# A hybrid state-space and attention block: norms' Newton steps moved between engines, and one state's feed a step made by another engine

## The chip, the cores and the metric

The kernel runs on one core of a Trainium2 chip. A core has a matrix engine (PE, whose weight loads are listed as PEld), a vector engine (DVE), an activation engine (ACT), a general engine (POOL) and an engine that here only issues transfers (SP). Each works through its own instructions in the order in which the program lists them, and waits for others by semaphores. The metric is the device time of one execution in microseconds (us).

## What is computed

Eight pictures of 64 x 64 tokens with 96 channels go through two layers.

```python
# layer 0: group norm, then a four-direction state-space scan
xz = x @ in_proj_w.T ; xh, z = split(xz)
xc = silu(depthwise_conv3x3(xh) + conv_b)
xs = [diagonal, anti-diagonal, and both reversed]            # K=4 orders of the 4096 tokens
dts, Bs, Cs = split(xs @ x_proj_weight)
delta = softplus(dts @ dt_projs + bias)
def step(hst, inp):                                           # 192 channels, 16 states each
    u_t, d_t, B_t, C_t = inp
    hst = hst * exp(d_t[..., None] * A) + (d_t * u_t)[..., None] * B_t
    return hst, einsum(hst, C_t)
y = sum of the directions, in picture order, + Ds * xs
yn = layernorm(y) * ln_w + ln_b
x = x + yn * silu(z) @ out_proj_w.T
# layer 1: attention without a softmax, then a quantized feed-forward net
t = t + attention(layernorm(t))
t = t + ffn(layernorm(t))                                     # weights and inputs in 8-bit floats
```

## The kernel before

**Scan.** The 192 channels of two directions lie as three groups (g) of 128 partitions. A picture takes 16 steps: eight chunks of 512 tokens forward, then the same eight backward. A step runs over 16 states, so the main loop in `run` has 8 x 16 x 16 = 2048 turns, one state each. For a state n of a step m:

- `decay` (line 966): ACT makes exp(delta * A), three instructions, two turns ahead, into one of three buffers. A buffer is free again when DVE's scan three states before is done.
- the feed, delta * u * B, comes in one of three ways, by the letter in `FEED` for that state. For "A", ACT scales the transposed delta * u by B (line 988, eight instructions), and for "G" POOL does the same in three (line 979); both two turns ahead (`times_b`), into one of two buffers, and PE then transposes it with twelve matmuls into three PSUM banks (`turn`, line 996). For "D", PE spreads B's row over the partitions with one matmul (line 998), and DVE multiplies it by delta * u, three products (line 1013), just ahead of the scans.
- `recur` (line 1009): DVE scans the three groups. Between the second and the third scan it gives other work a place, `work.at("V")`.
- `keep` and `read` (lines 1025, 1030): one turn later POOL stores the carry and multiplies h by C.
- `reduce` (line 1044): four turns later PE adds it up over states and transposes it, in PSUM.

**Prologue of a step.** `prologue` makes delta, du (delta * u, line 928, POOL, one buffer) and its transpose duT for the step after next. du is made only when the step in hand has used the old one for the last time, which is told by `n == FEED.rindex("D")` in `recur`. The Softplus (line 921) needs another table in ACT, so two table loads go with it.

**Side work.** The stages before and after the scan of a picture run as jobs in the gaps of the main loop: `front` of picture b + 1 (norm, convolution, reordering) in the first half of picture b's steps, `measures` (group norm's statistics) of b + 2, and `tail` of b - 1 in the second half. A job is a generator; each `yield` names the engine of its next piece and a cost in us. `Work.at` lets a piece in when the engine's credit allows it; `LAGS` says how many turns must lie between pieces on different engines. After ACT, a POOL piece may go in the same turn ("AG": 0) and a DVE piece one turn later ("AV": 1); from POOL to PE, and from DVE to ACT, it is one turn, and from DVE to PE the last place of the same turn. In turn 7 of the next picture (`at == LAG + 3`) all that is left is issued at once.

**Tail.** For each of 8 chunks of 512 tokens, `join` adds the directions, takes a layer norm (n) that ACT applies, multiplies by the gate, projects, and takes a second layer norm (a), which POOL applies (lines 698 to 700), for attention's Gram matrix. When all are joined, `attention` makes one 96 x 96 matrix, and `layers` applies it, takes a third norm (f), which POOL applies (line 799), and runs the feed-forward net; its hidden values are cast to 8 bits by DVE (line 819). A chunk c is joined only when c - 2 is. The last picture's tail runs after the scans, all chunks side by side.

**Norm.** `rsqrt` (lines 395 to 412) gets mean and variance, takes variance to the power -1/2 by ACT's logarithm and exponential, and sharpens it by one Newton step on POOL (lines 405 to 411), which also gives -mean * r. Its tensors have 4 numbers a partition (one for each 128 tokens), or 1 for the group norm (line 466), whose results are copied to `at.norm`.

Of the kernel before, what the change touches and what calls it, by code (L numbers as in the profile page):

```python
# [13 lines left out]
ALU = mybir.AluOpType  # L14
# [6 lines left out]
DM = 96  # L21
# [23 lines left out]
DOUBLE = 2 * WW * DI  # L45
WIDE = 3 * WW * DI

FEED = "DADADAGADADAAAAA"


@with_exitstack
# [189 lines left out]
def dve(us, lag=None):  # L241
    return "V", us, lag, False


def gp(us, lag=None):
    return "G", us, lag, False
# [149 lines left out]
def rsqrt(nc, pool, k, mv, p, n, tag):  # L396

    r = pool.tile([p, n], F32, tag=tag + "r", name=tag + "r")
    s = pool.tile([p, n], F32, tag=tag + "s", name=tag + "s")
    m = pool.tile([p, n], F32, tag=tag + "m", name=tag + "m")  # L400
    yield act(0.4)
    nc.scalar.activation(r, mv[:, :, 1], AF.Ln, bias=k.eps[:p])
    nc.scalar.activation(r, r, AF.Exp, scale=-0.5)
    yield gp(1.0)
    nc.gpsimd.tensor_scalar(m, mv[:, :, 1], 1e-5, -0.5, ALU.add, ALU.mult)
    nc.gpsimd.tensor_tensor(s, r, r, ALU.mult)
    nc.gpsimd.tensor_tensor(s, s, m, ALU.mult)
    nc.gpsimd.tensor_scalar(s, s, 1.0, 1.5, ALU.mult, ALU.add)
    nc.gpsimd.tensor_tensor(r, r, s, ALU.mult)
    nc.gpsimd.tensor_tensor(m, mv[:, :, 0], r, ALU.mult)  # L410
    nc.gpsimd.tensor_scalar(m, m, -1.0, 0.0, ALU.mult, ALU.add)
    return r, m


# [13 lines left out]
def measures(tc, work, pool, x, k, at, b):  # L428

    nc = tc.nc  # L430
# [12 lines left out]
    def aggregate():  # L443
        mv = pool.tile([DM, 2], F32, tag="mv", name="mv")
        yield dve(0.4)
        nc.vector.bn_aggr(mv, stats.rearrange("p c s -> p (c s)"))

        ps = yield bank(0.1)
        v = view(ps, DM, 1)
        nc.tensor.matmul(v, k.group, mv[:, 0:1], start=True, stop=True)  # L450
        gmv = pool.tile([DM, 1, 2], F32, tag="gmv", name="gmv")
        yield act(0.2)
        nc.scalar.copy(gmv[:, :, 0], v)
        work.release(ps)
        dev = pool.tile([DM, 1], F32, tag="dev", name="dev")
        yield gp(0.6)
        nc.gpsimd.tensor_tensor(dev, mv[:, 0:1], gmv[:, :, 0], ALU.subtract)
        nc.gpsimd.tensor_tensor(dev, dev, dev, ALU.mult)
        nc.gpsimd.tensor_tensor(dev, dev, mv[:, 1:2], ALU.add)
        ps = yield bank(0.1)  # L460
        v = view(ps, DM, 1)
        nc.tensor.matmul(v, k.group, dev, start=True, stop=True)
        yield act(0.2)
        nc.scalar.copy(gmv[:, :, 1], v)
        work.release(ps)
        r, m = yield from rsqrt(nc, pool, k, gmv, DM, 1, "g")
        nc.gpsimd.tensor_copy(at.norm[:, 0:1], r)
        nc.gpsimd.tensor_copy(at.norm[:, 1:2], m)
        at.measured = True

    yield [aggregate()], 1
# [136 lines left out]
def tail(tc, work, x, out, k, at, b, last=False):  # L608


    nc = tc.nc
    area = dict(reuse_waits="tile")
    with tc.tile_pool(name=f"t1_{b}", bufs=1, **area) as p1:
# [5 lines left out]
        with tc.tile_pool(name=f"t2_{b}", bufs=8 if last else 2, **area) as p2:  # L619
# [3 lines left out]
            def join(c):  # L623
                s = slice(4 * c, 4 * c + 4)
# [69 lines left out]
                    nc.vector.bn_aggr(mv[:, i, :], st[:, i, :])  # L694
                r, m = yield from rsqrt(nc, p2, k, mv, P, 4, "a")
                xa = ys[0].rearrange("p a c -> p (a c)")[:, 0 : 4 * (DM + 1)].rearrange("p (a c) -> p a c", a=4)
                yield gp(1.6)
                nc.gpsimd.memset(xa[:, :, DM : DM + 1], 1.0)
                for i in range(4):
                    nc.gpsimd.tensor_scalar(xa[:, i, 0:DM], t[:, i, :], r[:, i : i + 1], m[:, i : i + 1], ALU.mult, ALU.add)  # L700


                ps = yield bank(0.65)
# [58 lines left out]
        with tc.tile_pool(name=f"t3_{b}", bufs=8 if last else 3, **area) as p2:  # L762

            def layers(c):
# [5 lines left out]
                if last:  # L770
                    t, xaT = kept[c]
# [22 lines left out]
                    nc.vector.bn_aggr(mv[:, i, :], st[:, i, :])  # L794
                r, m = yield from rsqrt(nc, p2, k, mv, P, 4, "f")
                xf = tile("xf", [P, 4, DM])
                yield gp(1.4)
                for i in range(4):
                    nc.gpsimd.tensor_scalar(xf[:, i, :], t[:, i, :], r[:, i : i + 1], m[:, i : i + 1], ALU.mult, ALU.add)

                ps = yield bank(0.45)
                v = view(ps, DM, CH)
# [477 lines left out]
```

## Time and profile before

| | us |
|---|---|
| median of 3 runs | 11244.71 (11232.78 to 11246.39) |
| profiled execution, span | 11243.9 |
| first scan of the loop | 244.2 |
| end of the last scan | 10996.3 |

Busy time over the whole span, of the lines that the change touches or stands next to:

```
L1009 DVE  scan h             6514.2 us in 5376, 879.5 us in 768
L966  ACT  decay              3975.0 us in 6144
L988  ACT  feedT              3673.7 us in 10240
L1044 PE   y                  3847.4 us in 24576
L928  POOL du                  448.4 us in 128
L1025 POOL carry               402.5 us in 2048
L799  POOL xf, scaling         107.0 us in 256
L700  POOL xa, scaling         106.1 us in 256
L405 to L411 POOL, norm f       96.9 us in 448
L405 to L411 POOL, norm a       89.3 us in 448
L405 to L411 POOL, norm n       89.1 us in 448
```

Busy time is the time in which at least one instruction of the group ran; where instructions overlap in the engine's pipeline, their mean duration times their number is more. A line such as "idle before, releaser" tells how long the engine stood still before these instructions and whose end let it go on.

### The profile page before, as it was taken

The page shows a single profiled execution, that of the slowest core. Times are in us where ns is not written, and L with a number is a line of the kernel's source. Part 1 is how long each engine was busy: PE and PEld are TensorE (multiplying, and loading weights), DVE is VectorE, ACT ScalarE, POOL GpSimd, SP SyncE. Part 2 cuts the span into 40 slices and gives each one's busy share as a digit, 9 for nine tenths or more (in the row PEclk, how much of TensorE's full clock was granted, in tenths as well). Part 3 has the DMA queues.
Part 4 walks back from the last instruction along what each step waited for, and adds up shares of the span by engine and source line. Part 5 has one row for each costly group of instructions (what it writes and reads, how often), then busy time and mean ns, then how long its engine had stood idle before and what let it go on. Part 6 is the DMA issues. An engine that isn't in the chain of part 4 may idle for free.

```text
span 11243.9 us, 182845 instructions
## 1 busy us (share of the span) xinstructions
PE 9140.0 (81%) x60885; PEld 7661.4 (68%) x60885; DVE 9396.9 (84%) x10582; ACT 9455.9 (84%) x19651; POOL 9365.4 (83%) x7047
## 2 busy tenths in 40 slices
PE   6888788878888788878888788887888878878884
PEld 5677677666676667766677666776667666666663
DVE  2988988888888888888888888888898888989993
ACT  3888888888888888888888888888898888888883
POOL 1877987899878998789987899779997799998994
PEclk8999999888998889988999898998999988889886
DMA  3335333543335443354334543345433543432332
GB/s 91 106 92 143 100 98 92 144 118 102 97 93 149 110 108 95 96 144 113 102 92 113 138 107 102 92 118 134 109 99 90 133 119 104 108 103 84 99 94 63
DMA packets 1122742, 1206.98 MB, mean 107 GB/s; under 512 B 452790, under 2 KB 730007, under 8 KB 1121799
## 3 DMA queue, kind: packets, MB, share of 16 engines
q1 hardware_dynamic: 1121798, 1195.28, 40.3%
q8 instruction: 485, 7.95, 0.3%
q14 instruction: 459, 3.75, 0.1%
HBM read 874.83 MB, written 319.98 MB: 106 GB/s over the span
## 4 chain that ended last, share of the span: by engine, by line
PE 24%; ACT 23%; DVE 17%; POOL 14%; issue 10%; DMA 7%; SPq 4%; DVEq 0%; POOLq 0%; ACTq 0%
DVE h L1009 11%; ACT feedT L988 9%; POOL h L1030 8%; ACT decay L966 7%; PE y L1044 7%; PE feed L996 7%; DMA cc<-crow 4%; DVE feed L1013 4%; PE bank L542 3%; SPq L587 2%; PE bank L894 2%; PE feed L998 1%; ACT L63 1%; POOL du L928 1%; DMA y<-wide 1%
## 5 line engine op out<-in xcount | busy, mean ns | idle before, releaser
L1030 POOL TENSOR_TENSOR h<-h,cc 128x1536 f32<-128x1536 f32 x2048 | 7079.9, 3457 | 458.3 <-DMA cc<-crow 228.9
L1009 DVE TENSOR_TENSOR_SCAN h<-decay,carry,feed 128x512 f32<-128x512 f32 x5376 | 6514.2, 1262 | 810.2 <-PE feed L996 704.8
L966 ACT ACTIVATE decay<-delta,a_neg 128x512 f32<-128x512 f32 x6144 | 3975.0, 714 | 1116.4 <-DVE h L1009 1114.4
L996 PE MATMUL feed<-ident,feedT 128*128 128x128 f32 x16896 | 3090.8, 303 | 1649.1 <-DVE h L1009 1084.6
L1044 PE MATMUL y<-ident,h 128*128 128x128 f32 x24576 | 3847.4, 290 | 130.7 <-POOL h L1030 47.4
L996 PEld LDWEIGHTS feed<-ident,feedT 128*128 128x128 f32 x16896 | 2209.1, 155 | 2246.9 <-ACT feedT L988 840.8
L988 ACT ACTIVATE feedT<-duT,rows 128x192 f32<-128x192 f32 x10240 | 3673.7, 445 | 17.6 <-PE feed L996 14.7
L1044 PEld LDWEIGHTS y<-ident,h 128*128 128x128 f32 x24576 | 3164.5, 152 | 525.2 <-issue 410.3
L1013 DVE TENSOR_TENSOR feed<-feed,du 128x512 f32<-128x512 f32 x1920 | 1200.4, 685 | 162.2 <-PE feed L998 146.5
L1025 POOL COPY carry<-h 128x3 f32<-128x3 f32 x2048 | 402.5, 197 | 877.0 <-DVE h L1009 803.2
L1009 DVE TENSOR_TENSOR_SCAN h<-decay,feed 128x512 f32<-128x512 f32 x768 | 879.5, 1201 | 118.9 <-PE feed L996 106.8
L542 PE MATMUL bank<-wf,xp 97*128 97x192 f32 x4266 | 851.9, 332 | 0.0
L998 PE MATMUL feed<-x,pick 77*128 77x512 f32 x1280 | 708.8, 636 | 3.9
L542 PEld LDWEIGHTS bank<-wf,xp 97*128 97x128 f32 x4266 | 692.8, 194 | 5.4 <-issue 4.6
L928 POOL TENSOR_TENSOR du<-delta,u 128x1536 f32<-128x1536 f32 x128 | 448.4, 3503 | 188.8 <-ACT delta L921 188.8
L916 PE MATMUL bank<-x,ws 13*128 13x512 f32 x764 | 435.5, 650 | 5.6 <-ACT x L907 5.6
L979 POOL TENSOR_TENSOR feedT<-duT,rows 128x512 f32<-128x512 f32 x384 | 396.2, 1060 | 4.7 <-PE feed L996 4.7
L894 PE MATMUL bank<-wx,u 128*128 128x77 f32 x3048 | 360.0, 275 | 0.0
L894 PEld LDWEIGHTS bank<-wx,u 128*128 128x128 f32 x3048 | 352.3, 193 | 1.9 <-ACT duT L936 0.2
L918 DVE COPY delta<-bank 128x512 f32<-128x512 f32 x382 | 256.7, 672 | 86.5 <-PE bank L916 86.1
L934 PE MATMUL bank<-ident,du 128*128 128x128 f32 x1532 | 251.8, 291 | 65.1 <-POOL du L928 61.8
L998 PEld LDWEIGHTS feed<-x,pick 77*128 77x128 f32 x1280 | 211.5, 200 | 97.6 <-DVE h L1009 44.8
(261 smaller groups left out, 6957.4 us busy)
## 6 DMA issues: line engine op xcount, KB each, us to landing
cc<-crow SPq DMA_DIRECT2D x4096, 128.0 KB
u<-seq SPq DMA_DIRECT2D x256, 384.0 KB
wide<-ys SPq DMA_DIRECT2D x512, 192.0 KB
ut<-image SPq DMA_DIRECT2D x768, 64.0 KB
seq<-us SPq DMA_DIRECT2D x128, 384.0 KB
part<-ys SPq DMA_DIRECT2D x64, 768.0 KB
y<-part SPq DMA_DIRECT2D x64, 768.0 KB
y<-wide SPq DMA_DIRECT2D x256, 192.0 KB
```

What stands on the lines that cost most here:

```text
L542: nc.tensor.matmul(v[:, j, :], flat[:, o : o + P], k.wf[:, i, :], start=(i == 0), stop=(i == 8), skip_group_check=True)
L894: nc.tensor.matmul(v[:, j, :], u[:, g, j * P : (j + 1) * P], w.wx[:, q, g, :], start=(g == 0), stop=(g == G - 1))
L916: nc.tensor.matmul(ps, w.ws[:, q, g, :], x[0 : 2 * NR + 1, :], start=True, stop=True)
L928: nc.gpsimd.tensor_tensor(du, delta, u, ALU.mult)
L966: nc.scalar.activation(decays[i][:, g, :], made[m].delta[:, g, :], AF.Exp, scale=w.a_neg[:, q, g, n : n + 1])
L988: nc.scalar.activation(f[part], o.duT[part], AF.Copy, scale=o.rows[:, j, XB + d * NS + n : XB + d * NS + n + 1])
L996: nc.tensor.transpose(feed[g][:, j * P : (j + 1) * P], feeds[i][:, j * G + g, :], w.ident)
L998: nc.tensor.matmul(feed[0], w.pick[:, FEED[:n].count("D"), :], made[m].x, start=True, stop=True)
L1009: nc.vector.tensor_tensor_scan(h[:, g, back], a[:, g, back], feed[g][:, back], init, ALU.mult, ALU.add)
L1013: nc.vector.tensor_tensor(feed[g], feed[0], made[m].du[:, g, :], ALU.mult)
L1030: nc.gpsimd.tensor_tensor(hs[i], hs[i], c.unsqueeze(1).to_broadcast([P, G, T]), ALU.mult)
L1044: nc.tensor.matmul(y[:, j, :], hs[i][:, g, r * P : (r + 1) * P], w.ident, is_transpose=True, start=(n == 0 and j % 4 == 0), stop=(n == NS ...
```

## The change

Four edits in one. In `FEED`, D leaves states 4 and 10 and G leaves 6; 4 and 10 become G and 6 becomes D. `rsqrt`'s Newton step is written with four `scalar_tensor_tensor` on DVE, each two operations with two tensors, in place of seven instructions on POOL. The two copies of the group norm's result go to DVE, and so do the ones and the four scalings of a and the four of f.

```diff
-FEED = "DADADAGADADAAAAA"
+FEED = "DADAGADADAGAAAAA"
...
-    yield gp(1.0)
-    nc.gpsimd.tensor_scalar(m, mv[:, :, 1], 1e-5, -0.5, ALU.add, ALU.mult)
-    nc.gpsimd.tensor_tensor(s, r, r, ALU.mult)
-    nc.gpsimd.tensor_tensor(s, s, m, ALU.mult)
-    nc.gpsimd.tensor_scalar(s, s, 1.0, 1.5, ALU.mult, ALU.add)
-    nc.gpsimd.tensor_tensor(r, r, s, ALU.mult)
-    nc.gpsimd.tensor_tensor(m, mv[:, :, 0], r, ALU.mult)
-    nc.gpsimd.tensor_scalar(m, m, -1.0, 0.0, ALU.mult, ALU.add)
+    yield dve(0.45)
+    nc.vector.scalar_tensor_tensor(s, r, -0.5, r, ALU.mult, ALU.mult)
+    nc.vector.scalar_tensor_tensor(s, mv[:, :, 1], 1e-5, s, ALU.add, ALU.mult)
+    nc.vector.scalar_tensor_tensor(r, s, 1.5, r, ALU.add, ALU.mult)
+    nc.vector.scalar_tensor_tensor(m, mv[:, :, 0], -1.0, r, ALU.mult, ALU.mult)
...
-        nc.gpsimd.tensor_copy(at.norm[:, 0:1], r)
-        nc.gpsimd.tensor_copy(at.norm[:, 1:2], m)
+        nc.vector.tensor_copy(at.norm[:, 0:1], r)
+        nc.vector.tensor_copy(at.norm[:, 1:2], m)
...
-                yield gp(1.6)
-                nc.gpsimd.memset(xa[:, :, DM : DM + 1], 1.0)
+                yield dve(0.8)
+                nc.vector.memset(xa[:, :, DM : DM + 1], 1.0)
                 for i in range(4):
-                    nc.gpsimd.tensor_scalar(xa[:, i, 0:DM], t[:, i, :], r[:, i : i + 1], m[:, i : i + 1], ALU.mult, ALU.add)
+                    nc.vector.tensor_scalar(xa[:, i, 0:DM], t[:, i, :], r[:, i : i + 1], m[:, i : i + 1], ALU.mult, ALU.add)
...
-                yield gp(1.4)
+                yield dve(0.7)
                 for i in range(4):
-                    nc.gpsimd.tensor_scalar(xf[:, i, :], t[:, i, :], r[:, i : i + 1], m[:, i : i + 1], ALU.mult, ALU.add)
+                    nc.vector.tensor_scalar(xf[:, i, :], t[:, i, :], r[:, i : i + 1], m[:, i : i + 1], ALU.mult, ALU.add)
```

## The prediction

> **What bounds it now.** I read the busy shares and the chain of waits, then the costly groups, then two stretches instruction by instruction, and last the busy time by stage.
>
> ```profile
> PE 9140.0 (81%) x60885; PEld 7661.4 (68%) x60885; DVE 9396.9 (84%) x10582; ACT 9455.9 (84%) x19651; POOL 9365.4 (83%) x7047
> ...
> PE 24%; ACT 23%; DVE 17%; POOL 14%; issue 10%; DMA 7%; SPq 4%; DVEq 0%; POOLq 0%; ACTq 0%
> DVE h L1009 11%; ACT feedT L988 9%; POOL h L1030 8%; ACT decay L966 7%; PE y L1044 7%; PE feed L996 7%; DMA cc<-crow 4%; DVE feed L1013 4%; PE bank L542 3%; SPq L587 2%; PE bank L894 2%; PE feed L998 1%; ACT L63 1%; POOL du L928 1%; DMA y<-wide 1%
> ...
> L1030 POOL TENSOR_TENSOR h<-h,cc 128x1536 f32<-128x1536 f32 x2048 | 7079.9, 3457 | 458.3 <-DMA cc<-crow 228.9
> ...
> L996 PE MATMUL feed<-ident,feedT 128*128 128x128 f32 x16896 | 3090.8, 303 | 1649.1 <-DVE h L1009 1084.6
> ...
> L1013 DVE TENSOR_TENSOR feed<-feed,du 128x512 f32<-128x512 f32 x1920 | 1200.4, 685 | 162.2 <-PE feed L998 146.5
> ...
> L998 PE MATMUL feed<-x,pick 77*128 77x512 f32 x1280 | 708.8, 636 | 3.9
> ...
> L979 POOL TENSOR_TENSOR feedT<-duT,rows 128x512 f32<-128x512 f32 x384 | 396.2, 1060 | 4.7 <-PE feed L996 4.7
> ```
>
> No engine is the bound: four stand at 81 to 84% and the chain passes among all of them. So busy time saved counts only where its engine is the one waited for. Busy time over count, not the mean, prices overlapping instructions: a D state's three products on DVE (L1013) take 1200.4/640 = 1.88 us, a G state's three on POOL (L979) 396.2/128 = 3.10 us, one of PE's feed transposes (L996) 0.183 us, the D state's one matmul (L998) 0.553 us.
>
> The sum is made on this execution, span 11243.9 us; the median of the runs is 11244.7, so 0.8 us is added at the end.
>
> **The order of feeds.** Five D states a step become four, one G becomes two; A keeps its places 1, 3, 5, 7, 9 and 11 to 15, so ACT's work is the same. Per step DVE loses 1.88 us, POOL gains 3.10, PE gains 12 x 0.183 - 0.553 = 1.64. Over 128 steps: DVE -241, POOL +396, PE +210 us. But what is really done is that D leaves states 4 and 10 and comes to state 6. A step without side work, 2543 to 2618 us, shows which of these DVE is waited for in:
>
> ```profile
> 2569.35 1.28 DVE L1009 TENSOR_TENSOR_SCAN h<-decay,carry,feed 128x512 f32<-128x512 f32 x1 [0.59 <-PE feed L996]
> 2572.55 1.28 DVE L1009 TENSOR_TENSOR_SCAN h<-decay,carry,feed 128x512 f32<-128x512 f32 x1 [1.92 <-PE feed L996]
> ...
> 2592.64 1.87 DVE L1013 TENSOR_TENSOR feed<-feed,du 128x512 f32<-128x512 f32 x3
> ```
> ```profile
> 2589.24 1.95 ACT L966 ACTIVATE decay<-delta,a_neg 128x512 f32<-128x512 f32 x3 [2.91 <-DVE h L1009]
> ```
>
> The first two lines are state 5's scans: DVE stands idle before them for feeds that ACT, held by the Softplus block, made late. State 4's D lies just ahead of this stall, so the 1.88 us that it gives up are spent in it. The third line is state 10's D. ACT's decay at 2589.24 had waited 2.91 us for DVE's state 8; after it ACT runs without a gap to the step's end, so state 10's D already hides under ACT. State 6 lies between the stall and that decay, where ACT waits for DVE: there 1.88 us are lost. Ends: a loss of 241 us if every step is like this one; a gain of one D in five of what the chain holds (L1013 at 3.9% of the span, 439 us), 88. I take half the loss, +120: nearer to the step seen, but steps with side work are less regular.
>
> PE's 1.64 us count where PE is full: 315.1 of 354.5 us in the next picture's front (first line below), 28 such steps, 46 us. Ends 0 and 46; I take 23. Elsewhere its idle time covers them; in the tightest stretch they would be 1.64 a step. POOL's second G is issued in state 8, ahead of carry and h's product; du may now be issued there too, as the last D is state 8. PE's reduction, four states behind, is what waits if POOL falls so far back; it has POOL's next three products as slack.
>
> **The norms leave POOL.** Per chunk of 512 tokens there are three norms, per picture 8 chunks. POOL's seven steps are some 0.2 us each, 1.4 to 1.5 us a norm; the four scalings (L700, L799) take 1.66 us. So a joining chunk loses 2 x 1.4 + 1.66 + 0.11 (memset) = 4.6 us of POOL, a layer chunk 1.5 + 1.66 = 3.2.
>
> ```profile
> 1589.80:1944.30 354.50, 315.10 (x2105) 266.69 (x2104) 292.48 (x294) 299.70 (x587) 263.58 (x147) 0.98 0.35 94
> 2189.50:2543.00 353.50, 287.45 (x1957) 247.47 (x1956) 298.53 (x394) 301.93 (x651) 330.04 (x327) 0.88 0.44 115
> 2618.40:2885.20 266.80, 215.30 (x1424) 176.37 (x1424) 236.72 (x277) 232.09 (x490) 245.03 (x215) 0.89 0.38 102
> ```
>
> These rows are window, then busy PE, weight load, DVE, ACT, POOL: four front steps, four joining steps, three layer steps. POOL is fullest in the last two (330.0 of 353.5; 245.0 of 266.8). Joins give back 8 x 4.6 - 4 x 3.1 = 24 us a picture, layers 8 x 3.2 - 3 x 3.1 = 16: together 40, in seven pictures 280. ACT at 302 and DVE at 299 stand close behind, so I take a third, -93; ends 0 and -280.
>
> **They come to DVE.** The double operation with two inputs is not in the trace before. Bounds: L177 below, two inputs of three elements, 155 ns; a dependent aggregate (L655), 182 ns. I take 170. A scaling is nearest L119, 96 elements, 259 ns, taken as 250.
>
> ```profile
> L119 DVE TENSOR_SCALAR tap<-turned,conv_w 96x96 f32<-96x96 f32 x18 | 4.0, 259 | 0.1
> ...
> L177 DVE TENSOR_TENSOR both<-dd 128x3 f32<-128x3 f32 x1 | 0.2, 155 | 0.0
> ```
>
> A chunk adds 12 x 0.17 + 8 x 0.25 + 0.06 = 4.1 us, 56 chunks in the loop 230 us. DVE's idle time in the joins is 55 us and in the layers 30; the additions here (8 x (8 x 0.17 + 4 x 0.25 + 0.06) = 19 and 8 x (4 x 0.17 + 1) = 13) with the next term's (8 x 4 x 1.28 = 41 and 8 x 2 x 1.28 = 20), less the freed D (4 and 3 times 1.88), come to 52 and 27, so they fill it nearly, and idle time made by other engines can't all be refilled. Half is exposed: +115, ends 0 and 230. They sit between a state's second and third scan, so what queues behind them is that third scan, and behind it PE's next feed, POOL's carry and ACT's next decay.
>
> **The wait that the change adds.** One DVE instruction in the loop has both ends in SBUF at a fast rate, the cast of hq:
>
> ```profile
> 2872.07 2.59 DVE L819 CAST hq<-h 128x1536 fp8e5<-128x1536 f16 x1 [0.64 <-ACT h L816]
> ```
> ```profile
> 2870.41 3.44 POOL L1030 TENSOR_TENSOR h<-h,cc 128x1536 f32<-128x1536 f32 x1
> 2873.80 0.91 POOL L1025 COPY carry<-h 128x3 f32<-128x3 f32 x1
> ```
> ```profile
> L819 DVE CAST hq<-h x64: 931/1938/4025, 2662.0 to 11224.9; 128x1536 fp8e5<-128x1536 f16 x64
> ```
>
> The cast, 0.96 us where POOL is idle, lasts 2.59: POOL's product ends at 2873.85 and the cast 0.81 later. POOL's carry, 0.19 elsewhere, lasts 0.91, to the moment the cast is over. One keeps the other out. The scans, which take one operand from PSUM, keep to 1.26 us all along. The mean of the 64 casts is 2.084 us; without eight at the end at 0.96 it is 2.245, so 1.28 us lost each. POOL works about nine tenths of the time in these stretches, nearly always on products of 3.46 us.
>
> The Trainium skill, SBUF — State Buffer, Who interferes with whom, says so as a rule, and it speaks against this change: GpSimd and DVE's second port pair share one exclusive lock, taken by copies and tensor_scalar in two-port modes and, against a GpSimd that reads SBUF, by DVE instructions with two SBUF inputs; the loser waits for the whole instruction. By it all twelve double operations and eight scalings of a chunk are lock takers; by the trace only the cast is shown, and no row has a double operation beside a busy POOL. By the rule with every taker paying the cast's price the term below would be 1434 us.
>
> How often it is paid is unknown. Lower end: never (too short, or POOL idle), 0. Upper end: each of 20 x 56 = 1120 instructions pays 1.28, 1434 us. In between: after one has been let in, POOL takes its next product, and the one behind waits again until POOL has caught up, about a product behind. I take two payments a norm, six a chunk: 56 x 6 x 1.28 = 430, half exposed as above, +215.
>
> **The last picture's end** (10996 to 11244 us) has no scans, and POOL's norms are a chain there: eight chunks 3.74 us apart (one norm and its scalings), twice. On DVE a chunk takes 4 x 0.17 + 4 x 0.25 = 1.7, with gram's sum or xq's cast 2.0 to 2.4: 8 x 1.7 = 14 and 8 x 1.4 = 11 saved, and some 3 in the first norms: -28, ends -15 and -40.
>
> **Sum.** 120 + 23 - 93 + 115 + 215 - 28 = +352: 11243.9 + 352 + 0.8 = 11597 us.
>
> Not priced: a norm read by ACT now comes one state later in the hand-made order, and of the eight joins each pair waits for the one before: four states later. The last layer chunk, now in state 2 of the next picture, moves to about 6; state 7 empties the queue by force. Beyond it, some 10 us a picture.
>
> **Rivals.** *Order alone, the port hardly counts*: too short to be caught. Without the 215 the time is 11382. For it: no row shows short ones caught. Against: POOL's 0.2 us steps beside a cast do stretch, to 0.81. *Every one pays*: joins then add 8 x 12 x 1.28 = 123 us to DVE, layers 8 x 8 x 1.28 = 82, seven pictures 1435, nearly all exposed as DVE overflows its stretch: about 12500 us. Against: POOL runs out of products once DVE holds up the scans. *The balance works (faster)*: relief of POOL decides, in joins and layers. The D that is gone gives 88, POOL 93, the end 28, DVE's new work lies in its idle time: 11244.7 - 209 = 11036 us. For it: POOL is 93% busy there. It decides as soon as the lock costs under about 0.2 us an instruction and state 6 lies off the path. Against: the 2.91 us wait. *That it does nothing*: the terms cancel.
>
> **Chances.** Forecast 0.50 (its own range 11450 to 11800), order alone 0.20, every one pays 0.10, faster 0.17, nothing 0.03. Time: 11597. The range from 11220 (leaves out most of the faster case) to 12000 (leaves out most of every one pays). A change within 0.2%, 22 us, can't be told from none: faster 0.16, same 0.04, slower 0.80.
>
> **What will show it.** Port: the scalings at L700 and L799's successors on DVE average well over 0.26 us, up to 3.5, ending some 0.1 to 0.3 us after a POOL product; if they average 0.25 the term is wrong. Order: in the clean step ACT's wait for DVE before state 11's decay grows from 2.9 to some 4.8 us, and the step from 75 to 77; if it gets shorter, that step is wrong. POOL's busy time falls by 396 - 495 = -100 us, of which 495 is 275 of steps and 220 of scalings. The end shortens by 28 us of 248. I am wrong if the joining steps get shorter than 353.5 us.

## The result, and the profile after

The changed kernel takes 12046.67 us (median of 4 runs, 12033.21 to 12054.52), the kernel before 11245.55 (11232.78 to 11250.71) beside it: a ratio of 1.0711, 95% interval 1.0696 to 1.0726. The profiled execution spans 12031.4 us, 787.5 more than before. The forecast was 11597, with a range up to 12000: the side was right, and the loss more than twice what was worked out.

First the busy shares and two groups from the page of the changed kernel (busy us; in a group: busy time, mean ns of one, idle time before it and what ended it). Line numbers behind the Newton steps are three lower than before.

```profile
PE 9551.9 (79%) x62165; PEld 8026.1 (67%) x62165; DVE 9864.2 (82%) x11588; ACT 9463.9 (79%) x19651; POOL 9256.2 (77%) x5439
...
L1006 DVE TENSOR_TENSOR_SCAN h<-decay,carry,feed 128x512 f32<-128x512 f32 x5376 | 6524.7, 1262 | 1263.2 <-PE feed L993 1050.3
...
L963 ACT ACTIVATE decay<-delta,a_neg 128x512 f32<-128x512 f32 x6144 | 3974.9, 713 | 1799.7 <-DVE h L1006 1798.3
```

The same two groups in the kernel before:

```profile
L1009 DVE TENSOR_TENSOR_SCAN h<-decay,carry,feed 128x512 f32<-128x512 f32 x5376 | 6514.2, 1262 | 810.2 <-PE feed L996 704.8
L966 ACT ACTIVATE decay<-delta,a_neg 128x512 f32<-128x512 f32 x6144 | 3975.0, 714 | 1116.4 <-DVE h L1009 1114.4
```

POOL's busy time fell by 109 us (forecast 100), DVE's rose by 467 and PE's by 412, and all four shares are still close together, a little lower: no engine has become full, and what grew is the waiting of each for the others. The scans stand idle 1263 us before they start, 1050 of them for PE's feeds, and ACT's decays 1800 us, nearly all for the scans. The mean granted clock of the matrix engine is 0.888, before 0.907, and its two largest groups of matmuls last 306 and 293 ns each, before 303 and 290; what part of the loss that carries, no run shows.

The same stages as in the prediction, by windows (start and end, length, then busy PE, weight loads, DVE, ACT and POOL, granted clock, DMA share, GB/s): four front steps, four joining steps, the step with hardly any side work (the quiet step), three layer steps, the last picture's end.

```profile
1653.00:2021.80 368.80, 330.29 (x2180) 285.80 (x2179) 286.49 (x281) 299.35 (x587) 275.00 (x159) 0.95 0.33 90
2282.40:2672.60 390.20, 302.51 (x1993) 259.79 (x1992) 348.13 (x485) 298.35 (x642) 312.16 (x181) 0.86 0.38 105
2672.60:2752.90 80.30, 66.03 (x442) 54.05 (x440) 67.93 (x72) 67.30 (x145) 64.25 (x40) 0.91 0.33 90
2752.90:3042.00 289.10, 217.30 (x1445) 178.19 (x1443) 259.77 (x326) 230.19 (x486) 231.42 (x138) 0.88 0.35 94
11802.80:12031.40 228.60, 107.47 (x592) 75.31 (x590) 88.71 (x392) 80.98 (x182) 44.09 (x30) 0.63 0.30 63
```

The front steps have no norms to speak of, and yet they went from 354.5 to 368.8: that is the order of feeds (with the norms alone, `e2_norms` below, the same window takes 354.2). The joining steps went from 353.5 to 390.2, the quiet step from 75.4 to 80.3, the layer steps from 266.8 to 289.1. Only the end got shorter, 247.6 to 228.6.

That POOL and DVE keep each other out, as forecast, can be read instruction by instruction from the timeline of the changed kernel (start, length, engine, line). A norm's four double operations on DVE:

```profile
2763.35 0.95 DVE L405 SCALAR_TENSOR_TENSOR fs<-fr 128x4 f32<-128x4 f32 x1
2764.33 0.16 DVE L406 SCALAR_TENSOR_TENSOR fs<-mv,fs 128x4 f32<-128x4 f32 x1
2764.53 3.42 DVE L407 SCALAR_TENSOR_TENSOR fr<-fs,fr 128x4 f32<-128x4 f32 x1
2767.98 0.98 DVE L408 SCALAR_TENSOR_TENSOR fm<-mv,fr 128x4 f32<-128x4 f32 x1
```

and POOL in the same few microseconds:

```profile
2760.84 3.45 POOL L1027 TENSOR_TENSOR h<-h,cc 128x1536 f32<-128x1536 f32 x1
2764.22 0.19 POOL L1022 COPY carry<-h 128x3 f32<-128x3 f32 x1
2764.49 3.44 POOL L1027 TENSOR_TENSOR h<-h,cc 128x1536 f32<-128x1536 f32 x1
```

The first double operation ends with POOL's product (2764.30 and 2764.29), the second runs free in 0.16 us beside a carry, and the third, four numbers a partition, lasts 3.42 us, as long as POOL's next whole product. This is the wait that the prediction priced, seen now on instructions for which the trace of before had no row. The Trainium skill, SBUF — State Buffer, Who interferes with whom, says that GpSimd (POOL) and DVE's second port pair share one exclusive lock; the row agrees, also for so short a taker.

### The profile page after: what moved, and what is told of

Read it like the earlier page. It is cut to its first block, busy times and chain, and to the rows that moved or that the text cites. A ratio compares the mean times of both kernels' runs of the same rounds, so it can differ in the third digit from the quotient of the medians.

```text
span 12031.4 us, 184972 instructions
## 1 busy us (share of the span) xinstructions
PE 9551.9 (79%) x62165; PEld 8026.1 (67%) x62165; DVE 9864.2 (82%) x11588; ACT 9463.9 (79%) x19651; POOL 9256.2 (77%) x5439
## 5 line engine op out<-in xcount | busy, mean ns | idle before, releaser
L993 PE MATMUL feed<-ident,feedT 128*128 128x128 f32 x18432 | 3464.7, 306 | 1968.8 <-DVE h L1006 1291.3
L993 PEld LDWEIGHTS feed<-ident,feedT 128*128 128x128 f32 x18432 | 2432.7, 156 | 2744.7 <-ACT feedT L985 978.9
L1041 PE MATMUL y<-ident,h 128*128 128x128 f32 x24576 | 3947.1, 293 | 128.8 <-ACT ys L1064 125.6
L1041 PEld LDWEIGHTS y<-ident,h 128*128 128x128 f32 x24576 | 3213.7, 154 | 460.5 <-issue 285.7
L1010 DVE TENSOR_TENSOR feed<-feed,du 128x512 f32<-128x512 f32 x1536 | 961.2, 686 | 156.6 <-PE feed L995 156.3
L976 POOL TENSOR_TENSOR feedT<-duT,rows 128x512 f32<-128x512 f32 x768 | 799.9, 1069 | 13.8 <-PE feed L993 13.7
L995 PE MATMUL feed<-x,pick 77*128 77x512 f32 x1024 | 567.8, 637 | 0.8
L891 PE MATMUL bank<-wx,u 128*128 128x77 f32 x3048 | 442.1, 312 | 42.3 <-DMA u<-seq 32.5
L891 PEld LDWEIGHTS bank<-wx,u 128*128 128x128 f32 x3048 | 435.3, 230 | 45.2 <-issue 28.0
L1077 POOL TENSOR_TENSOR ys<-ys,y 128x768 f32<-128x768 f32 x128 | 233.0, 1821 | 67.3 <-ACT ys L1064 67.2
L931 PE MATMUL bank<-ident,du 128*128 128x128 f32 x1532 | 251.4, 290 | 39.2 <-POOL du L925 38.9
```

Source lines behind the costliest of these rows:

```text
L891: nc.tensor.matmul(v[:, j, :], u[:, g, j * P : (j + 1) * P], w.wx[:, q, g, :], start=(g == 0), stop=(g == G - 1))
L976: nc.gpsimd.tensor_tensor(f.rearrange("p (j g) (d c) -> p g j d c", g=G, d=d)[:, g], o.duT.rearrange("p (j g) (d c) -> p g j d c", g=G, d= ...
L993: nc.tensor.transpose(feed[g][:, j * P : (j + 1) * P], feeds[i][:, j * G + g, :], w.ident)
L995: nc.tensor.matmul(feed[0], w.pick[:, FEED[:n].count("D"), :], made[m].x, start=True, stop=True)
L1010: nc.vector.tensor_tensor(feed[g], feed[0], made[m].du[:, g, :], ALU.mult)
L1041: nc.tensor.matmul(y[:, j, :], hs[i][:, g, r * P : (r + 1) * P], w.ident, is_transpose=True, start=(n == 0 and j % 4 == 0), stop=(n == NS ...
```

## The experiments

Each was timed in 3 to 5 rounds beside the kernel before (median 11232.76 to 11242.88 in the five groups of runs); "slower by" is the difference of the medians taken together.

### The two halves apart

`e1_order`, the new order of feeds alone:

```diff
-FEED = "DADADAGADADAAAAA"
+FEED = "DADAGADADAGAAAAA"
```

> The kernel before with the new order of feeds alone (norms stay on POOL). Theory port (most of the 801 us is DVE waiting for POOL in the norms; the order costs at most the 1.88 us a step of the prediction): at most +241 us, about 11365 to 11490. Theory order (the steps without a norm grew by 2 to 9 us in the changed kernel too, so the new place of D and G costs about 4.4 us in each of 128 steps): +450 to +600 us, about 11700 to 11850.

Measured: 11846.15 us, slower by 613 (ratio 1.0543, 1.0527 to 1.0558). The prediction had 143 for it (120 and PE's 23); what the second G loads onto POOL it had put into the norms' terms, as less relief.

`e2_norms`, the changed kernel with the old order of feeds:

```diff
-FEED = "DADAGADADAGAAAAA"
+FEED = "DADADAGADADAAAAA"
```

> The changed kernel with the old order of feeds: norms and their scalings on DVE, FEED as before. Theory port: +550 to +700 us, about 11800 to 11950. Theory order: +200 to +350 us, about 11450 to 11600. Under both the double operations and scalings on DVE last as long as in the changed kernel, some 700 us together; if the two parts are additive, the two runs' losses sum to 801 us.

Measured: 11684.8 us, slower by 452 (1.0402, 1.0386 to 1.0417), between the two ranges, where the terms of the norms gave 209. The halves add up to 1065, 264 more than the whole change's 801. So two things are to be explained: the order's 470 beyond the forecast, and why the norms cost more alone than in company.

### Inside the order of feeds

`e4_swap` exchanges D and G between states 4 and 6, `e3_last` turns state 10's D into a G.

```diff
-FEED = "DADADAGADADAAAAA"
+FEED = "DADAGADADADAAAAA"   # e4_swap
+FEED = "DADADAGADAGAAAAA"   # e3_last
```

> The kernel before with D and G of states 4 and 6 exchanged, D stays at 10, so no engine's work changes. The prediction's reading: state 4's D hid in the stall at state 5, state 6's D doesn't hide: +1.88 us a step, +241 us, 11486. Theory order: the stall at state 5 grows by what state 4 gave up and more: +241 to +500 us. If state 6 is off the path: no change.

> The kernel before with only the last D state (10) made a G state; G stays at 6, D at 0, 2, 4, 8. Prediction's reading (state 10's D hides under ACT): within 30 us of before on that account. Theory order says that a second G close behind the first, and du let go two states earlier, load POOL, and that PE has 1.64 us more a step: +0 to +200 us. A gain would be up to 88 us.

Measured: the swap 11386.03, slower by 153 (1.0134, 1.0118 to 1.0149), close to the forecast's 120 and below both theories of this run; state 10 alone 11759.12, slower by 526 (1.0469, 1.0451 to 1.0487), 4.1 us a step on average, far above the range. The two together come to 679, 66 more than the whole order's 613: they are not quite additive.

State 10's letter does two things. It gives POOL a second G, and since `recur` lets go of du at `n == FEED.rindex("D")`, it moves du's product on POOL from turn 10 to turn 8. `e5_last_gate` keeps the first and undoes the second:

```diff
-FEED = "DADADAGADADAAAAA"
+FEED = "DADADAGADAGAAAAA"
...
-        if n == FEED.rindex("D"):
+        if n == 10:
```

> e3_last (state 10 from D to G, alone, +526 us) with du let go in turn 10 again, as before the change, instead of turn 8. Theory du: du is issued two turns earlier, directly behind the new G on POOL, and PE, in order, stands at du's transposes (PE waits for du: 61.8 us before, 260.8 in e3_last) and feeds DVE late. Then most of the loss goes: +0 to +150 us, 11235 to 11385. Theory load: the second G's 3.1 us on POOL and 1.64 us on PE cost it by themselves: still +350 to +550 us.

Measured: 11431.72, slower by 192 (1.0167, 1.0150 to 1.0184), between the two ranges. So 335 of the 526 us come from du being let go two turns earlier, with not one instruction more or fewer, and 192 from the G in place of a D, with PE's transposes that go with it. Steps measured from their first scan to the next step's, as means over the second to the seventh picture, show where these 192 lie: of 24.8 us a picture, 21.7 in the last eight steps, 2.7 a step, where the tail runs and the G takes 3.10 us of a POOL that is nearly full.

The expected symptom of du was wrong, though. Here are lines from the waits (who waits for whom: us, times, longest) of the kernel before,

```profile
DVE h L1009 <- PE feed L996: 811.6, 729, 4.4
...
PE bank L934 <- POOL du L928: 61.8, 35, 3.6
...
ACT duT L936 <- PE bank L934: 47.7, 47, 2.0
```

of `e3_last`,

```profile
DVE h L1009 <- PE feed L996: 1464.1, 1039, 14.2
...
PE bank L934 <- POOL du L928: 260.8, 75, 6.7
...
ACT duT L936 <- PE bank L934: 223.2, 95, 7.5
...
PE bank L894 <- DMA u<-seq: 56.9, 13, 9.2
```

and of `e5_last_gate`:

```profile
DVE h L1009 <- PE feed L996: 1054.9, 863, 7.6
...
PE bank L934 <- POOL du L928: 243.7, 80, 7.6
...
ACT duT L936 <- PE bank L934: 81.8, 80, 4.9
```

PE waits for du about as long in both. What differs is who waits behind PE: ACT, for du's transposes, 223.2 against 81.8 us, and DVE, for feeds, 1464.1 against 1054.9. The last line of `e3_last`, PE's wait for the load of u, has none beside it in `e5_last_gate` or in the kernel before. POOL's timeline in one step of `e3_last` shows how du comes late:

```profile
4111.32 3.46 POOL L1030 TENSOR_TENSOR h<-h,cc 128x1536 f32<-128x1536 f32 x1
4114.74 3.09 POOL L979 TENSOR_TENSOR feedT<-duT,rows 128x512 f32<-128x512 f32 x3
4117.77 0.19 POOL L1025 COPY carry<-h 128x3 f32<-128x3 f32 x1
4118.04 3.47 POOL L1030 TENSOR_TENSOR h<-h,cc 128x1536 f32<-128x1536 f32 x1
4121.46 3.47 POOL L928 TENSOR_TENSOR du<-delta,u 128x1536 f32<-128x1536 f32 x1
```

and DVE's, what stands behind it:

```profile
4115.26 10.65 DVE L1009 TENSOR_TENSOR_SCAN h<-decay,carry,feed 128x512 f32<-128x512 f32 x9
4127.70 2.45 DVE L1009 TENSOR_TENSOR_SCAN h<-decay,carry,feed 128x512 f32<-128x512 f32 x2 [1.79 <-PE feed L996]
```

Between them stands PE:

```profile
4124.99 0.66 PE L934 MATMUL bank<-ident,du 128*128 128x128 f32 x4 [1.38 <-POOL du L928]
4125.48 0.81 PE L779 MATMUL bank<-t,ident 128*128 128x384 f32 x2
4126.13 1.03 PE L784 MATMUL bank<-w_att,xaT 97*128 97x96 f32 x8
4126.99 0.60 PE L996 MATMUL feed<-ident,feedT 128*128 128x128 f32 x4
```

The second G (3.09 us), a product and du queue up on POOL without a gap; du ends at 4124.93, and PE, which has du's transposes ahead of the next feeds in its queue, goes on only then. But two pieces of a layer (lines 779 and 784) stand in between as well, and the feeds begin only at 4126.99. DVE had run nine scans on feeds made earlier, and then stands for 1.79 us.

That letting du go in turn 8 costs 335 us is measured; this path to it is read from the waits and was not tested by itself, and a rival stands. With du the side work moves: by the kernels' own scheduling the first picture's last join is issued six turns earlier in `e3_last` than in `e5_last_gate` (485 against 491 in the table below). Of the 43 us by which a picture is longer in `e3_last` (means as above), the third, sixth, eighth and thirteenth step hold 35, while the seventh is 7 shorter; the sixth is also the one in which PE waits most for the load of u, 6 us on average. No run moves du and keeps the side work in place, so how the 335 divide among du's queue, the load of u and the side work stays open. In the whole changed kernel PE waits only 38.9 us for du, and ACT 60.8 for its transposes.

`e6_after_gate` makes the same one-line edit in the changed kernel:

```diff
-        if n == FEED.rindex("D"):
+        if n == 10:
```

> The whole changed kernel with du let go in turn 10 instead of turn 8. Theory du: 250 to 450 us of the 801 come back, about 11600 to 11800. Theory load: no more than 100 us come back.

Measured: 11896.53, slower by 657 (1.0579, 1.0564 to 1.0595). Only 145 of the 801 us come back, not 250 to 450: a miss, which is taken up below.

### Inside the norms

`e7_newton` moves only the Newton steps to DVE, `e8_scale` only the scalings, the ones and the group norm's copies:

```diff
-    yield gp(1.0)
-    nc.gpsimd.tensor_scalar(m, mv[:, :, 1], 1e-5, -0.5, ALU.add, ALU.mult)
...
+    yield dve(0.45)                                    # e7_newton
+    nc.vector.scalar_tensor_tensor(s, r, -0.5, r, ALU.mult, ALU.mult)
...
-                yield gp(1.6)
+                yield dve(0.8)                         # e8_scale
...
-                    nc.gpsimd.tensor_scalar(xa[:, i, 0:DM], t[:, i, :], r[:, i : i + 1], m[:, i : i + 1], ALU.mult, ALU.add)
+                    nc.vector.tensor_scalar(xa[:, i, 0:DM], t[:, i, :], r[:, i : i + 1], m[:, i : i + 1], ALU.mult, ALU.add)
```

> The kernel before with the Newton steps alone on DVE; the scalings stay on POOL, FEED as before. Theory port (every double operation is a taker of the port; in the changed kernel they were 550 us of DVE's 704 us of norm work): +250 to +400 us of e2_norms' +452. Rival: the latency (ACT to DVE is one turn later, and POOL must wait for DVE before it scales) costs, not the port; then DVE's double operations get shorter here, under 0.3 us each, and the loss is still there.

> The kernel before with the scalings (and the ones and the group norm's copies) alone on DVE; Newton's seven steps stay on POOL. Theory port: the eight scalings a chunk cost 150 us of DVE with waits in the changed kernel, so +50 to +200 us. If scalings that follow each other keep the port (0.35 us each there), near +50; if relief of POOL outweighs it, a gain of up to 60 us.

Measured: Newton alone 11500.26, slower by 260 (1.0228, 1.0213 to 1.0244); scalings alone 11534.97, slower by 295 (1.0260, 1.0245 to 1.0275), above what was expected. Together they would be 555, the norms as a whole cost 452. The group of the scalings in `e8_scale` (busy, mean ns):

```profile
L700 DVE TENSOR_SCALAR y<-t,ar,am 128x96 f32<-128x96 f32 x256 | 263.0, 1088 | 26.7 <-POOL am L411 26.5
```

and in the changed kernel, where double operations run ahead of them:

```profile
L697 DVE TENSOR_SCALAR y<-t,ar,am 128x96 f32<-128x96 f32 x256 | 77.9, 368 | 1.2
```

A scaling too is kept out by POOL, if it comes first: 1088 ns against 368. Behind four double operations it hardly waits. The reading is that the double operations have let POOL's backlog run off by then; it was not tested.

Two runs put idle instructions into the kernel before, ahead of POOL's Newton steps of each norm: `e9_idle_double` four double operations, `e10_idle_single` four that read one tensor.

```diff
+    if tag != "g":
+        yield dve(0.45)
+        nc.vector.scalar_tensor_tensor(q, mv[:, :, 1], -0.5, mv[:, :, 0], ALU.mult, ALU.mult)   # e9, and three alike
...
+        for _ in range(2):                                                                      # e10
+            nc.vector.bn_stats(q, mv.rearrange("p a b -> p (a b)"))
+            nc.vector.bn_aggr(z, q)
```

> The kernel before, with four more instructions on DVE in each norm of the pictures' ends, whose results nobody uses: double operations with two tensors from SBUF, of the changed kernel's shape, in its place between the scans. Nothing else moves. Theory port (a DVE instruction with two inputs in SBUF waits until POOL's product is done): they average 0.4 to 0.8 us in place of 0.16, and the kernel loses 150 to 350 us. Rival (any four small instructions there cost it, by their count and the turn's delay): the same loss as e10_idle_single.

> As e9_idle_double, but the four are batch-norm statistics and aggregates, which read one tensor. Theory port: they keep to 0.15 to 0.25 us each, some 140 us of DVE in all, and the kernel loses 0 to 100 us, clearly less than e9_idle_double. Rival: both lose the same.

Measured: 11541.64, slower by 303 (1.0272, 1.0258 to 1.0286), and 11365.98, slower by 128 (1.0114, 1.0101 to 1.0128), somewhat above its range. Two groups of the first:

```profile
L407 DVE SCALAR_TENSOR_TENSOR nq<-mv 128x4 f32<-128x4 f32 x64 | 77.0, 1203 | 0.0
L408 DVE SCALAR_TENSOR_TENSOR nq<-mv,nq 128x4 f32<-128x4 f32 x64 | 38.5, 601 | 2.2
```

and two of the second:

```profile
L410 DVE BATCH_NORM_AGGREGATE nz<-nq 128x2 f32<-128x6 f32 x128 | 23.3, 182 | 4.4
L409 DVE BATCH_NORM_STATS2 nq<-mv 128x6 f32<-128x8 f32 x128 | 20.3, 159 | 2.2
```

At the same place, e9's twelve groups average 163 to 1203 ns, 553 over all 768, the longest 3.44 us; e10's average 159 and 182, and none is longer than 0.18 us. They differ in the operation too, not only in the number of tensors read. All of e9's idle instructions are busy 424.5 us, e10's 130.3. But e10's 128 us for 130 of work looked like full payment, on an engine that has idle time in every stage. That asked for a control.

### The places in the program

An added `yield` is not free even when nothing is issued in it. After ACT, a DVE piece may come one turn later and a POOL piece in the same turn, so the norms on DVE push every join back. Following the kernels' own scheduling turn by turn gives the turn (by the scheduling's own count, which starts before the loop) in which the first picture's last join is issued, and the pieces of a later picture that are still open in turn 7 of the next one and are then all issued at once:

```
kernel                                  last join   pieces issued at once
before, e4_swap, e5_last_gate, e8_scale    491          0
e1_order, e3_last                          485          0
the changed kernel                         490          0
e17_order_later                            488          0
e2_norms, e6_after_gate                    500         30
e13_turn_later, e18_gate_later             500         28
e7_newton                                  502         38
e9_idle_double, e10_idle_single,
  e14_empty_turn                           502         40
```

The new order pulls the joins six turns forward, since du is let go earlier (state 10's letter does it alone, and not with du late); the norms push them back; the changed kernel comes out where it was. With the old order, or with du late, the side work with the norms' later places no longer fits into a picture's 256 turns. Four controls make such places without norm work on DVE: `e13_turn_later` for the norms alone, `e14_empty_turn` for e9 and e10, with nothing in their place, `e17_order_later` for the changed kernel, and `e18_gate_later` for it with du late. (Their expectations count turns in the second picture, where the 7 or 8 rounds of issuing at once are counted too: 763 there is 9 turns later, not 16.)

```diff
-    yield gp(1.0)
+    yield gp(1.0, 1 if tag == "n" else None)       # e13; e17 and e18 with the new FEED, e18 also with "if n == 10:"
...
+    if tag != "g":                                 # e14, ahead of the unchanged yield gp(1.0)
+        yield dve(0.45)
```

> The kernel before, with the first layer norm's Newton steps (n) let out on POOL one turn later than before; no instruction is added, removed or moved to another engine. In the program's order this puts the joins of a picture where the norms on DVE alone put them (the last join 16 turns later than before) and leaves 28 pieces of the layers to be issued at once in turn 7 of the next picture, where before leaves none. Theory, the timetable: much of the 452 us of the norms alone comes from these later places, so this run is 100 to 250 us slower, 15 to 25 us of it a picture in the first step of the next picture and some 12 in the step that had no side work. Rival, DVE's work and waits alone: 0 to 40 us slower.

> The kernel before, with the place that the idle instructions had on DVE ahead of the Newton steps of n, a and f kept, but with nothing issued in it: the control for both runs with idle instructions. Theory, the timetable: nearly all of the 128 us of the one-input instructions is the place, so this is 80 to 130 us slower. Rival, that small instructions between the second and third scan are paid in full: 0 to 40 us slower.

> The kernel before with the new order of feeds, and the first layer norm (n) let out on POOL one turn later. The joins then stand within two turns of where the changed kernel has them (last join 744, there 746; with the order alone 741; before 747), nothing is left over for turn 7 of the next picture, and no norm work is on DVE: the control for the changed kernel. Theory: the order pulls the joins forward and so takes in the later turn, the place costs nothing here, 600 to 650 us slower than before, and the norms' work and waits on DVE are the rest up to 801. Rival, that the later turn costs its 142 beside the new order too: 740 to 780.

> The same with du let go in turn 10: the joins stand where the changed kernel with du let go in turn 10 has them (last join 763) and 28 pieces are left for turn 7 of the next picture; no norm work is on DVE. Theory, the sum of the parts: the swap 153, state 10's G with du late 192 and the later turn 142, so 430 to 540 us slower than before; against the run before this the 335 of du's late release are then mostly eaten by the 142. Rival, that du's release is worth only some 150 where the swap is made too: 590 to 660.

Measured: e13 11384.86, slower by 142 (1.0126, 1.0112 to 1.0139); e14 11350.19, slower by 107 (1.0089, 1.0076 to 1.0103); e17 11836.79, slower by 602 (1.0533, 1.0519 to 1.0548); e18 11590.35, slower by 356 (1.0313, 1.0299 to 1.0327), below what was expected.

Where e13 loses it, the windows show: the third picture's first step and its twelfth, the last joining step, each from its first scan to the next step's, in the kernel before,

```profile
2888.01:2961.75 73.74, 59.69 (x394) 50.48 (x393) 66.58 (x67) 67.03 (x142) 69.94 (x43) 0.88 0.39 100
3826.88:3911.06 84.18, 72.16 (x484) 59.76 (x485) 73.22 (x92) 76.30 (x166) 81.00 (x73) 0.90 0.39 103
```

and in e13:

```profile
2892.16:2984.61 92.45, 67.92 (x439) 53.56 (x438) 71.12 (x86) 75.32 (x159) 78.11 (x68) 0.85 0.30 83
3844.05:3942.43 98.38, 72.93 (x473) 61.42 (x472) 75.80 (x100) 74.49 (x162) 88.43 (x84) 0.84 0.39 106
```

They grow by 18.7 and 14.2 us; as means over the second to the seventh picture by 14.9 and 13.0, while the other fourteen steps together get 6 shorter. The quiet step, into which the last join now runs, does not grow (75.0, before 76.1), though the run's expectation had some 12 us for it. The first step takes in pieces of layers that before were done earlier. DVE's timeline in that step of e13 shows the pieces that are issued at once:

```profile
2926.67 1.20 DVE L1009 TENSOR_TENSOR_SCAN h<-decay,feed 128x512 f32<-128x512 f32 x1
2937.23 0.69 DVE L807 CAST xq<-bank 96x512 fp8e5<-96x512 f32 x1 [9.35 <-PE bank L804]
2938.96 0.96 DVE L819 CAST hq<-h 128x1536 fp8e5<-128x1536 f16 x1 [1.04 <-ACT h L816]
2944.18 0.96 DVE L819 CAST hq<-h 128x1536 fp8e5<-128x1536 f16 x1 [4.26 <-ACT h L816]
2945.06 3.44 DVE L1009 TENSOR_TENSOR_SCAN h<-decay,feed 128x512 f32<-128x512 f32 x3
```

From 2927.87 to 2945.06 there is no scan: the casts stand ahead of the next scan in DVE's queue, and wait for a chain over PE and ACT.

Five points follow.

- `e7_newton`'s 260 have such a place in them, `e8_scale`'s 295 have not.
- The one-input idle instructions cost 128 - 107 = 21 us, about what these medians can tell from nothing; the double ones 303 - 107 = 196, of 424.5 us busy. A little under half is exposed.
- In the changed kernel's own places, the norms' work on DVE costs 801 - 602 = 199 us, give or take some 24 by the two intervals. The prediction's terms for it gave 209.
- The parts add up, by the way they are taken apart. The later turn is 142 us in the norms alone and is not paid in the whole change; the work in such places costs 452 - 142 = 310 there against 199 here; the order is 613 alone and 602 in these places. 142 + 111 + 11 = 264. Why the work is dearer in those places was not tried.
- `e6_after_gate` gave back little: with the norms, du's late release sends the side work over the picture's edge. In such places e18 is 246 us faster than e17, not 335, and the norms' work costs 657 - 356 = 301, not 199.

`e15_norms_in_place` and `e16_gate_in_place` tried the reverse: the norms on DVE in the same turn as ACT's exponential, so that the last join stays where it was (491, none left over), with the old order and with the new one and du late.

```diff
-    yield dve(0.45)
+    yield dve(0.45, 0)
```

> The norms and scalings on DVE with the old order of feeds, as in the run of the norms alone, but let in without the extra turn after ACT, so that every join and layer has the place in the program that it has before. Theory, the timetable: 150 to 300 us slower than before, not 452, and the first step of a picture as long as before. Rival, DVE's work and waits: 400 to 460.

> The changed kernel with du let go in turn 10 and the norms let in without the extra turn. Theory: du's early release is worth some 335 us also here, and the run with du let go in turn 10 hid that behind pieces issued at once; this run is 450 to 580 us slower than before, against 657 there. Rival, that du's release is worth only some 150 beside the norms: 640 to 670.

Measured: e15 11702.37, slower by 459 (1.0406, 1.0392 to 1.0420), e16 11922.92, slower by 680 (1.0601, 1.0587 to 1.0616). The theory misses in both: e15 ends in its rival's range, e16 above both. The edit brings a wait of its own. From the waits of e15:

```profile
DVE fs L405 <- ACT fr L403: 79.3, 35, 4.6
DVE as L405 <- ACT ar L403: 73.3, 37, 3.5
...
DVE ns L405 <- ACT nr L403: 31.2, 24, 3.6
```

DVE stands 183.8 us for ACT's exponentials, more than the later turn costs; the turn between ACT and DVE has its reason. These two runs tell nothing of the places, and no version of the norms on DVE in the loop was found that has neither the later turn nor this wait.

### The end by itself

`e11_end` gives DVE the Newton steps and scalings only in the last picture's tail, where no scans run; `e12_end_all` adds the gate's product and the last two sums there.

```diff
+    if quiet:                                          # rsqrt is called with quiet=last
+        yield dve(0.45)
+        nc.vector.scalar_tensor_tensor(s, r, -0.5, r, ALU.mult, ALU.mult)
...
+                yield dve(0.8) if last else gp(1.6)
+                e = nc.vector if last else nc.gpsimd
...
+                yield dve(1.2) if last else gp(2.3)    # e12
+                (nc.vector if last else nc.gpsimd).tensor_tensor(yg, yg, gate, ALU.mult)
```

> The kernel before with the changed norms and scalings in the last picture's end alone, where no scan runs and POOL holds no long product; the loop stays as before. Theory port: DVE's double operations last 0.16 us there, the end gets 15 to 25 us shorter (changed kernel: 228.6 us after the last scan, before 247.6), 11215 to 11230, a gain of 0.1 to 0.2%. If the scans' end or DMA bounds the end: no change.

> e11_end with POOL's gate product and its two last sums of the end on DVE too. POOL's eight gate products take 18.5 us in a row there and the last sums 14.6; on DVE a product of 1024 elements should take some 1.2 us (768 take 0.96). Gain over e11_end 8 to 18 us: 11200 to 11220, the fastest version. If ACT's chain behind them bounds the end: no more than 3 us.

Measured: 11210.5 us, 28 faster than before (0.9978, 0.9969 to 0.9987), and 11205.64, 33 faster (0.9975, 0.9965 to 0.9984). The second adds nothing that these intervals can tell, though 8 to 18 were expected; in the profiled executions its end is 217.4 us, e11's 227.9. e11 is the part of the change that is worth keeping, and both beat both kernels. Its norm and scaling groups in the end:

```profile
L407 DVE SCALAR_TENSOR_TENSOR ns<-mv,ns 128x4 f32<-128x4 f32 x8 | 1.3, 162 | 0.3
L708 DVE TENSOR_SCALAR y<-t,ar,am 128x96 f32<-128x96 f32 x32 | 8.4, 326 | 0.2
```

Here POOL has little to do (busy 42.7 of 227.9 us), and the double operation takes 162 ns, as priced (170).

## Why the prediction was right or wrong

**The order of feeds: the step that failed.** "State 10's D already hides under ACT" ended the account of that state: du's new turn got no term ("it has POOL's next three products as slack"), and the second G's 3.10 us stand in the sum only as less relief for POOL, four and three of them a picture, which at a third and over seven pictures is some 51 us. State 10's letter by itself cost 526 us: 335 for du's turn (`e5_last_gate` against `e3_last`) and 192 for the G with PE's transposes. The working looked at what the D had cost DVE (whether that D was hidden, no run shows by itself); it did not price what its replacement puts into POOL's queue, nor what else moves when du does. The slack named was that of PE's reduction. What waits longer with du in turn 8 is ACT for du's transposes (223 us against 82), DVE for feeds (1464 against 1055) and PE for the load of u (57 against none), and the side work stands in other turns; how the 335 divide among these stays open.

**State 6's D, +120:** near in size; the swap cost 153. Half of 1.88 us a step was a fair choice.

**PE's 23:** nearer to its lower end, 0. `e5_last_gate` has the same added transposes with du in its old turn, and its four front steps, where PE is fullest, are 0.4 us longer than before (means over the second to the seventh picture). The 14.3 us by which they grew in the changed kernel are the swap's and du's: the swap alone makes them 7.1 longer, du's turn (`e3_last` less `e5_last_gate`) 11.2.

**DVE's added work and the port, 115 + 215 less 93:** right as a sum; the 93 was not measured by itself. The changed kernel's double operations in n, a and f are busy 550.2 us, its scalings 149.9, its ones 4.0: 704. Without the end, where they run free in about 4 us a chunk, that is 12.0 a chunk, against 4.1 + 6 x 1.28 = 11.8. The payments are spread otherwise than thought: against the free 0.16 us the 768 double operations lose 427 us, the scalings, at 0.263 each, only 15, since they come last. The sum of 442 was forecast as 430. "Half exposed" held as well for the idle ones, 196 of 424.5, and the whole of the norms cost 199 against 237 - 28 = 209. With the G's 51 us counted with the order, the forecast was 158 for the norms and 194 for the order, against 199 and 602.

**"Not priced":** the later turn of the norms' pieces was seen and put at some 10 us a picture, should the side work run beyond turn 7. It does in the norms alone, and costs 142 us there. In the changed kernel it does not, since du's early release pulls the joins forward. That this took no part was luck, not working.

**The end, -28:** the changed kernel's is 19 us shorter, `e11_end`, which changes nothing else, is 28 faster (15 to 35 by its interval), its end 20 shorter.

**The signs named:** POOL's busy time was as said. The quiet step grew to 80.3 us and not 77, with ACT's waits for DVE in it split in two, 1.72 and 1.87 us, where one of 4.8 was expected: the stall was not where the forecast had put it. The scalings were to show the port with a mean well over 0.26; they show 0.37 and 0.34, and it is the double operations, at 0.72, that carry it.

**The rivals.** *The balance works* falls with the loss of 801 us; what POOL's relief gave by itself was not measured. *Every one pays* falls: the scalings hardly pay, and 442 us are far from 1435. *Order alone, the port hardly counts* falls, since the port was paid; it was the order, though, that made three quarters of the loss (602 of 801).

## What to carry to other kernels

When an instruction is taken off one in-order queue and given to another, price what now stands behind it there, and look in the code for every release that is tied to its position: here a condition on the last "D" moved another product by two turns, and side work with it, and that cost more than the moved work. When work changes engine under a hand-made order, follow the order first, since a place that falls over the edge of its stage can cost as much as the work (142 us against 199); and a control that keeps the place and issues nothing tells the two apart.

## What was unexpected of the hardware

A DVE instruction on four numbers a partition, 0.16 us by itself, lasted up to 3.44 us beside POOL's products of 3.45, and several in a row can each pay: the 768 of them averaged 0.72 us. Batch-norm statistics and aggregates of about that size, which read one tensor, were never caught at the same place (159 and 182 ns); scalings were, 1088 ns on average where no double operation stood ahead of them.
